# Attention and deformable attention in one kernel: three own taps in other units, the opening's loads on other queues, one late weight in later quarters

## The chip, the cores and the metric

The kernel runs on one core of a Trainium2 chip. Everything is float32. The metric is the device time of one execution in microseconds (us). A profile of one execution is read for the reasons: its span goes from the first to the last instruction. The engines are named PE (TensorE), DVE (VectorE), ACT (ScalarE), POOL (GpSimd) and SP (SyncE, which only issues DMAs). DMAs are issued from the queues of SP, ACT and POOL, each in its own program order.

## The reference

Two layers over `x` of 8 x 32 x 32 x 512, that is 8 batches of 1024 tokens with 512 channels:

```
# layer 0, per batch (seq = 1024 tokens, 8 heads of 64)
x_norm = group_norm(x)                        # 32 groups of 16 channels
q, k, v = split(x_norm @ w_qkv + b_qkv)
w   = softmax((q / 8) @ (k / 8).T)            # per head, 1024 x 1024
x   = x + (w @ v) @ w_out + b_out

# layer 1, per half batch of the reshaped image
x_ln = layernorm(x).transpose(0, 3, 1, 2)
q    = x_ln.reshape(...) @ wq + bq
o    = gelu(depthwise_conv_7x7_stride_2(q as an image) + dw_b)   # 49 taps a channel
off  = conv_1x1(o); grid = clip-free positions from tanh(off)
interp = bilinear samples of x at grid        # 256 points a batch
v = k = interp @ wv + bv
z   = softmax(qh @ kh.T) @ vh @ mo_w + mo_b + x       # heads of q, k, v by mq, mk, mv
out = gelu(layernorm(z) @ mlp_w + mlp_b) + z
```

## The kernel before

**Order.** Every instruction of an engine stands in the order in which the program issues it (the class `InOrder`, whose helper line, 54, is the line that most of the profile shows; tiles are therefore the names to go by). The order is written out by hand: `at(place, step)` puts a step on a list with a number as its due place, and `run_due(until)` runs all steps due before `until`, sorted by place and, where places are equal, by the order in which they were put down.

**Units.** Layer 0 is 256 units, 32 a batch (`per` = 32): a unit is one tile of 128 queries for one pair of heads. `push` (line 206) issues a unit: PE's scores into two `sc` tiles (`scores`, line 97), DVE's two row maxima `nmax`, ACT's two exponentials `e`; then the steps due before the unit's place 0.8; then DVE's two block transposes of `e` into `sq`; and, in odd units, sixteen DMAs on SP's queue that carry `sq` to `et` (`moved`, line 222); then the steps due before the next unit. There are two `sc` tiles, so the scores of a unit wait until ACT has read those of the unit before. The product of `et` with the values (`part`, tile `av`) follows three and four units after its odd unit. Units are numbered here from 0 to 31 within a batch, batches from 0 to 7.

**Work between.** The places around a batch hold the projections of q, k and v (`qkv_steps`, `value_steps`), the group norm of the next batch (`norm_steps`, line 582: `turn` transposes x into `xT`, `two_tiles` takes its statistics, `norm` applies them), and the output of the batch before (`out_steps`, line 739: on DVE `xr`, its statistics, `hat`; on POOL the sum with the bias and the two passes of `hat` over 128 x 512). In layer 0 there also runs the depthwise convolution of layer 1 for batches 0 to 5 (`EARLY` = 6): `conv_chunk` (line 950) does one block of 128 channels of one batch, and `conv_plan` (line 1000) says in which units its 49 taps fall. A row `(44, 6, 3)` means: in unit 44, counted from the start of the batch behind the block's own (so unit 12 of the batch after that), six taps by ACT and POOL (ACT scales into `part_x`, POOL adds to `oa`) and three by DVE alone (a SCALAR_TENSOR_TENSOR on `od`). DVE's own taps are due at 0.86 of their unit, so they come after the transposes of `sq` and ahead of the next unit's `nmax`. The blocks with own taps in the units that the change touches are the second (`cb` = 1, units 1 to 8) and the third (`cb` = 2, units 10 to 16) of each of those six batches; these parts of both run in batches 2 to 7.

**Opening.** Batch 0 has its eight tiles of x in two rows (lines 532 to 537): the first four, which are turned first, come by POOL's queue, the other four by SP's. The three thirds of `w_qkv` go to `wA` (queries), `wB` (keys) and `wC` (values), all by SP's queue, keys first (lines 547 and 548). The list `first_norm_places` (line 1032), shifted by -100, orders the first group norm; `warm(3)` (line 1050) puts matmuls without use at two places between. The squares of x for batch 1 (`load_squares`, line 523, four DMAs of 64 KB a tile, on POOL's queue) are due at `places[t] + 0.001`, right behind the first two turns (line 684); `load_weight(w_out)` on POOL's queue follows at -72.5.

**End of layer 0.** In batch 7 `fold_steps` (line 831) multiplies weights of layer 1 together. `load_quarter(w_out, c)` brings `w_out` back into the one tile `w` in four DMAs on ACT's queue at 25.2, 25.7, 26.2 and 26.7 (line 876); quarters of `mv_w` follow on the same queue at 27.2, 27.9, 28.6 and 29.3. The tile is read again at 33.1, after the last unit, by `out` of the last batch.

Of the kernel before, what the change touches and what calls it, by code (L numbers as in the profile page):

```python
# [17 lines left out]
P = 128  # L18
# [3 lines left out]
C = 512  # L22
NC = C // P
# [3 lines left out]
NQT = QB // P  # L27
NH = 8
HD = 64
# [219 lines left out]
def attention_then_deformable_attention(  # L249
# [30 lines left out]
    nc = tc.nc  # L280
    x_tok = x.rearrange("b h w c -> b (h w) c")
# [8 lines left out]
    ident = const.tile([P, P], F32, tag="ident", name="ident")  # L290
# [7 lines left out]
    def mm_tile():  # L298
        return ps_mm.tile([P, QB], F32, tag="mm", name="mm")
# [9 lines left out]
    def load_cols(pool, v, name):  # L309
        t = pool.tile([P, v.shape[0] // P], F32, tag=name, name=name)  # L310
        with nc.allow_non_contiguous_dma(reason="a vector onto partitions"):
            nc.sync.dma_start(t, v.rearrange("(c p) -> p c", p=P))
        return t
# [54 lines left out]
    def at(place, step):  # L368
        due.append((place, len(due), step))
# [40 lines left out]
    def kept(name):  # L410
        return keep.tile([P, NC, C], F32, tag=name, name=name)
# [98 lines left out]
    with ExitStack() as l0:  # L510
# [3 lines left out]
        nc = InOrder(tc)  # L514
        NX = 2
        NX_T = 3
        xs = {}
# [5 lines left out]
        def load_squares(b, t, r):  # L523
            if r == 0:
                xs[b, t] = work.tile([P, C], F32, tag="x", name="x", bufs=NX)
            nc.gpsimd.dma_start(
                xs[b, t][ts(r, SQ)].rearrange("q (s c) -> q s c", s=NSQ),
                x_tok[b][ts(t, P), ts(r, P)].rearrange("(s q) c -> q s c", s=NSQ),
            )
# [2 lines left out]
        x2 = work.tile([P, NC, QB], F32, tag="xT", name="x2", bufs=NX_T)  # L532
        for t in range(NQT):
            xs[0, t] = work.tile([P, C], F32, tag="attT", name="x0", bufs=NQB * NHP)
            nc.gpsimd.dma_start(xs[0, t], x_tok[0][ts(t, P), :])
            xs[0, NQT + t] = x2[:, t, :]
            nc.sync.dma_start(xs[0, NQT + t], x_tok[0][ts(NQT + t, P), :])
        w3 = [kept(name) for name in ("wA", "wB", "wC")]

        def load_runs(v, name):  # L540
# [3 lines left out]

        gsc, gbi = load_runs(gn_scale, "gsc"), load_runs(gn_bias, "gbi")
        bqkv = load_cols(wp, b_qkv, "bqkv")
        for i in (1, 0, 2):
            nc.sync.dma_start(w3[i], w_qkv.rearrange("(p c) o -> p c o", c=NC)[:, :, ts(i, C)])
        bout = load_row(wp, b_out, "bout")
        room_w = {}  # L550

# [5 lines left out]
        def load_quarter(w, c):  # L557
            if c == 0:
                room_w["w"] = work.tile([P, NC, C], F32, tag="w", name="w", bufs=1)
            nc.scalar.dma_start(room_w["w"][:, c, :], by_chunk(w)[:, c, :])  # L560
# [11 lines left out]
            out=g3, in_=g3, pattern=[[-span, ng], [0, span]], compare_op=ALU.is_ge,  # L572
# [3 lines left out]
            out=g3, in_=g3, pattern=[[span, ng], [0, span]], compare_op=ALU.is_ge,  # L576
# [5 lines left out]
        def norm_steps(b, start, places):  # L582
# [98 lines left out]
            if b + 1 < B:  # L681
                for t in range(NX):
                    for r, place in enumerate(square_places[NX + t]):
                        place = places[t] + 0.001 if b == 0 else place
                        at(start + place, lambda t=t, r=r: load_squares(b + 1, t, r))

        def qkv_steps(b, hp, places):

# [142 lines left out]
        def fold_steps(first):  # L831

            raws, wT = {}, {}

            rows = {}

            def row(name, dst, raw, vec):
                rows[name] = ByRow(dst, raws[raw], vec)

            def spare():  # L840
                return work.tile([P, NC, QB], F32, tag="xT", name="raw", bufs=NX_T)

            def fetch(name, w):
                raws[name] = spare()
                nc.gpsimd.dma_start(raws[name], by_chunk(w))

            def turn(name, m):
                if name == "v" and m == 0:
                    wT[name] = spare()
                src = room_w["w"] if name == "v" else raws["wq"]  # L850
                ps = mm_tile()
                for c in range(NC):
                    nc.tensor.transpose(ps[:, ts(c, P)], src[:, c, ts(m, P)], ident)
                nc.scalar.copy(wT[name][:, m, :], ps)

            def product(dst, tag, name, raw, i):
                if i == 0:
                    fold[dst] = kept(tag)
                ps = project(lambda m: wT[name][:, m, ts(i, P)], lambda m: raws[raw][:, m, :])
                nc.scalar.copy(fold[dst][:, i, :], ps)  # L860

            at(first + 18.3, number)
            for part in range(4):
                at(first + 18.35 + part, lambda part=part: load_biases(part))
            at(first + 19.3, set_refs)
            at(first + 17.7, lambda: load_weight(wv))
            at(first + 19.3, lambda: fetch("mk", mk_w))
            for m in range(NC):
                at(first + 23.5 + m // 2 + 0.05 * (m % 2), lambda m=m: turn("v", m))
            def quarter(name, w, c):  # L870
                if c == 0:
                    raws[name] = spare()
                nc.scalar.dma_start(raws[name][:, c, :], by_chunk(w)[:, c, :])

            for c in range(NC):
                at(first + 25.2 + 0.5 * c, lambda c=c: load_quarter(w_out, c))
                at(first + 27.2 + 0.7 * c, lambda c=c: quarter("mv", mv_w, c))
                at(first + per + 1.24 + 0.001 * c, lambda c=c: quarter("wq", wq, c))
            for i, place in enumerate((25.5, 27.5, 28.5, 29.5)):
                at(first + place, lambda i=i: product("wvk", "wC", "v", "mk", i))  # L880
            def row_tile():
                return work.tile([P, C], F32, tag="v", name="row_b", bufs=5)

            def col_tile():
                return work.tile([P, NC], F32, tag="mu", name="col", bufs=2)

            at(first + 24.65, lambda: row("k", bvk, "mk", bv_c))
            at(first + 24.651, lambda: rows["k"].away(row_tile(), nc.gpsimd))
            at(first + 27.9, lambda: rows["k"].back(col_tile(), nc.gpsimd))
            raws["wq"] = None  # L890

            for i, place in enumerate((30.5, 31.5, 32.5, 32.52)):
                at(first + place, lambda i=i: product("wvv", "wB", "v", "mv", i))
            last = first + per
            at(last + 0.6, lambda: wT.update(q=spare()))
            at(last + 2.41, lambda: rows["k"].add(nc.vector))
            at(last + 3.5, lambda: row("v", bvv, "mv", bv_c))
            at(last + 3.51, lambda: rows["v"].away(row_tile(), nc.scalar))
            at(last + 4.28, lambda: rows["v"].back(col_tile(), nc.scalar))
            at(last + 3.6, lambda: fetch("mq", mq_w))  # L900
            for m in range(NC):
                at(last + 4.27 + 0.001 * m, lambda m=m: turn("q", m))
            for i in range(NC):
                at(last + 4.5 + 0.01 * i, lambda i=i: product("wqq", "wA", "q", "mq", i))
            at(last + 4.48, lambda: row("q", bqq, "mq", bq_c))
            at(last + 4.481, lambda: rows["q"].away(row_tile(), nc.scalar))
            at(last + 4.515, lambda: rows["q"].back(col_tile(), nc.scalar))
            for name in ("v", "q"):
                at(last + 4.9, lambda name=name: rows[name].add(nc.vector))
# [40 lines left out]
        def conv_chunk(b, cb, n):  # L950
# [34 lines left out]
            for unit, by_scalar, by_vector in counts:  # L985
# [15 lines left out]
            (20.5, (24.3, 25.3),  # L1001
             ((26, 3, 2), (27, 4, 2), (28, 6, 3), (29, 6, 3), (30, 6, 2), (31, 6, 2), (32, 3, 1)), 32),
            (26.3, (32.3, 32.6),
             ((33, 6, 2), (34, 6, 2), (35, 4, 0), (36, 6, 3), (37, 4, 0), (38, 5, 0), (39, 4, 0),
              (40, 5, 2)), 41),
            (33.6, (41.3, 41.6),
             ((42, 6, 3), (43, 5, 1), (44, 6, 3), (45, 5, 1), (46, 5, 1), (47, 4, 0), (48, 6, 3)), 49),
            (42.6, (49.3, 49.6),
             ((50, 6, 2), (51, 6, 3), (52, 6, 3), (53, 5, 2), (54, 4, 1), (55, 4, 1), (56, 4, 2)), 56),
        ]  # L1010
# [39 lines left out]
        def warm(n):  # L1050
            out = mm_tile()
            for c in range(n):
                for m in range(2):
# [3 lines left out]
                        start=(c == 0), stop=(c == n - 1),  # L1057
                    )

        norm_steps(0, -100, first_norm_places)  # L1060
        for place in (-76.035, -74.5):
            at(place, lambda: warm(3))
        at(-72.5, lambda: load_weight(w_out))
# [15 lines left out]
        for b in range(B):  # L1079
            first = b * per  # L1080
            for hp in range(1, NHP):
                places = first_places if b == 0 else pair_places
# [20 lines left out]
            for hp in range(NHP):  # L1103
                for qt in range(NT):
                    n = first + hp * NT + qt
                    if n % per == 0 and b > 0:
# [6 lines left out]
                        if b + 1 == B:  # L1113
                            places = [last_places(B * per, t) for t in range(NT)]
                            out_steps(b, attT, places, last=True)
                    t = qkv[b, hp]
# [4 lines left out]
                        at=qt % NQT,  # L1121
# [8 lines left out]
    with ExitStack() as l1:  # L1130
        nc = tc.nc


        def pool(name, bufs=1):
            return l1.enter_context(tc.tile_pool(name=name, bufs=bufs, reuse_waits="tile"))

        late, late2, cv, cvhat, first, raw, wp = (
            pool(n) for n in ("late", "late2", "cv", "cvhat", "first", "raw", "w2")
        )
        work = pool("work1", 2)  # L1140
        nc = InOrder(tc)
# [404 lines left out]
        for hi in range(2 * B):  # L1546
            if hi > 1:
                for c, place in enumerate((-0.35, 0.65, 1.3, 1.65) if hi % 2 else (-0.7, 1.3, 1.65, 1.7)):
                    place = -1.03 if hi == 2 and c == 0 else place
# [39 lines left out]
```

## Time and profile before

| | |
|---|---|
| three runs | 3268.69, 3271.52 (median), 3274.23 us |
| the profiled execution | 3270.55 us, of which the span is 3268.8 us |
| layer 0 | about 34.6 to 2104 us of the span |
| busy | PE 3215.1, DVE 2544.7, ACT 1766.2, POOL 1633.5 us |
| DMA | 674.30 MB, mean 206 GB/s |
| first tile of x turned; first projection starts | 7.12; 23.30 us |
| PE's idle time, by what ended most of it | `sc` on ACT's `e` 10.8; `av` on the DMA into `et` 9.5; on the DMA of x 7.6 us |

How to read it: PE is busy nearly all the time, so the time is PE's own work plus the stretches in which it waits. A stretch is told by the interval between the starts of two units' scores (`sc<-k,q`). A unit takes PE 7.19 us without, and 10.62 us with a second projection, where nothing holds it up. A wait shorter than the drain of a matmul does not show as idle time, only as a longer interval.

### The profile page before, as it was taken

How to read it: one execution, taken by the hardware profiler on the slowest of the kernel's cores; microseconds unless marked ns; L12 is line 12 of the kernel's file. 1: busy time of each engine (PE TensorE's matmuls, PEld its weight loads, DVE VectorE, ACT ScalarE, POOL GpSimd, SP SyncE). 2: the span in 40 equal slices, each digit the busy share in tenths (PEclk: the TensorE clock that was granted, in tenths of full speed). 3: DMA queues.
4: the chain of work that ended last, by engine and by line, in shares of the span. 5: the costliest groups of instructions: out<-in, count | busy, mean ns of one | idle time of the engine just before them, and what ended most of it. 6: DMA issues, size and time to landing. Idle time of an engine off the chain costs nothing.

```text
span 3268.8 us, 59474 instructions
## 1 busy us (share of the span) xinstructions
PE 3215.1 (98%) x21476; PEld 1299.1 (40%) x21476; DVE 2544.7 (78%) x3493; ACT 1766.2 (54%) x3798; POOL 1633.5 (50%) x2110
## 2 busy tenths in 40 slices
PE   8999999999999999999999999999999999999999
PEld 4344444344344444444434434333333333333333
DVE  5777878898888888888888888457868687676765
ACT  3443356566567567557557656235555555554442
POOL 2002316755755765665674677225556565643323
PEclk9999999999999999999999999999999999999999
DMA  6666776777776776776676677678777786877874
GB/s 173 165 177 170 206 182 185 210 194 190 210 190 181 208 200 174 204 211 178 184 231 171 177 217 209 175 227 264 223 242 241 227 264 213 259 257 230 268 234 132
DMA packets 479900, 674.30 MB, mean 206 GB/s; under 512 B 77404, under 2 KB 269208, under 8 KB 479352
## 3 DMA queue, kind: packets, MB, share of 16 engines
q1 hardware_dynamic: 433760, 529.53, 56.6%
q0 software_dynamic: 42480, 136.79, 13.7%
q10 hardware_dynamic: 3368, 4.20, 0.4%
q8 instruction: 170, 2.79, 0.4%
q14 instruction: 122, 1.00, 0.1%
HBM read 263.17 MB, written 138.69 MB: 123 GB/s over the span
## 4 chain that ended last, share of the span: by engine, by line
PE 78%; ACT 5%; DVE 5%; POOL 5%; DMA 3%; issue 2%; SPq 1%; POOLq 0%; DVEq 0%; ACTq 0%
PE mm L54 49%; PE sc L54 15%; PE av L54 14%; ACT e L54 3%; POOL oa L54 2%; SPq L54 1%; DVE sq L54 1%; DVE nmax L54 1%; ACT part_x L54 1%; POOL xr L54 1%; DMA et<-sq_d 1%; POOL hat L54 1%; DMA et<-sq 1%; DVE chunk L54 1%; DMA sq_d<-sq 0%
## 5 line engine op out<-in xcount | busy, mean ns | idle before, releaser
L54 ACT ACTIVATE e<-sc,nmax 128x1024 f32<-128x1024 f32 (+1 forms) x1024 | 801.7, 796 | 534.7 <-DVE nmax L54 531.1
L54 DVE TENSOR_REDUCE nmax<-sc 128x1 f32<-128x1024 f32 (+1 forms) x640 | 749.5, 1212 | 272.1 <-PE sc L54 267.5
L54 POOL TENSOR_TENSOR oa<-part_x,oa 128x256 f32<-128x256 f32 x852 | 637.3, 748 | 534.9 <-ACT part_x L54 490.3
L54 DVE STREAM_TRANSPOSE sq<-e 128x1024 f32<-128x1024 f32 x640 | 764.1, 1224 | 119.9 <-ACT e L54 100.7
L54 ACT ACTIVATE part_x<-pad_x,dww_x 128x256 f32<-128x256 f32 x852 | 441.6, 545 | 282.4 <-POOL oa L54 280.5
L54 PE MATMUL sc<-k,q 64*64 64x512 f32 x4096 | 519.9, 602 | 12.3 <-ACT e L54 9.8
L54 PE MATMUL av<-et,v 128*64 128x256 f32 x4096 | 499.8, 386 | 16.4 <-DMA et<-sq 9.5
L54 PEld LDWEIGHTS av<-et,v 128*64 128x64 f32 x4096 | 274.9, 137 | 332.1 <-issue 159.2
L54 PEld LDWEIGHTS sc<-k,q 64*64 64x64 f32 x4096 | 140.5, 132 | 331.9 <-issue 214.4
L54 POOL TENSOR_TENSOR chunk<-parts,chunk 128x256 f32<-128x256 f32 x240 | 185.3, 772 | 137.2 <-ACT parts L54 123.5
L54 POOL TENSOR_TENSOR mv<-mv,minus_half 128x1 f32<-128x1 f32 x128 | 75.8, 593 | 327.7 <-DVE mv L54 326.6
L54 PE MATMUL mm<-wo,attH 128*64 128x512 f32 x1024 | 233.7, 598 | 0.0
L54 PE MATMUL mm<-wC,xT 128*64 128x256 f32 x2048 | 232.2, 379 | 0.0
L54 PE MATMUL mm<-xT,wB 128*64 128x512 f32 x1024 | 230.8, 592 | 0.6 <-DVE xT L54 0.6
L54 PE MATMUL mm<-hat_h,wA 128*64 128x512 f32 x1024 | 230.9, 593 | 0.0
L54 PE MATMUL mm<-xT,wA 128*64 128x512 f32 x1024 | 230.7, 592 | 0.0
L54 PE MATMUL mm<-w,attT 128*64 128x512 f32 x1024 | 230.1, 592 | 0.0
L54 DVE SCALAR_TENSOR_TENSOR od<-pad_x,dww_x,od 128x256 f32<-128x256 f32 x276 | 223.5, 810 | 5.5
L54 PE MATMUL mm<-wm,zT 128*64 128x512 f32 x976 | 220.7, 592 | 0.5 <-ACT zT L54 0.5
L54 ACT ACTIVATION_READ_ACCUMULATOR e<-sc,nmax 128x1 f32 x1024 | 209.6, 205 | 0.0
L54 POOL DMA_DIRECT2D x<-in_x_dram x144 | 80.5, 561 | 248.6 <-DVE xT L54 125.8
L54 PEld LDWEIGHTS mm<-wC,xT 128*64 128x64 f32 x2048 | 148.6, 137 | 77.1 <-issue 6.4
(200 smaller groups left out, 3590.5 us busy)
## 6 DMA issues: line engine op xcount, KB each, us to landing
et<-sq SPq DMA_DIRECT2D x2048, 128.0 KB
sq_d<-sq SPq DMA_DIRECT2D x128, 512.0 KB
et<-sq_d SPq DMA_DIRECT2D x128, 512.0 KB
inv<-rs_d SPq DMA_DIRECT2D x250, 128.0 KB
xr<-mid POOLq DMA_DIRECT2D x64, 256.0 KB
xr<-in_x_dram POOLq DMA_DIRECT2D x62, 256.0 KB
out_dram<-res POOLq DMA_DIRECT2D x60, 256.0 KB
zn_d<-zn SPq DMA_DIRECT2D x57, 256.0 KB
```

The lines of the kernel that those rows point to most:

```text
L54: return self.tc.keep_in_program_order(op(*args, **kwargs))
```

## The change

The change has five parts.

1. `conv_plan`: DVE's own taps move. In the second block one tap goes from unit 40 to unit 38 (batch units 8 and 6). In the third, one goes from unit 44 and two from unit 48 (batch units 12 and 16), two go to unit 45 and one to unit 47 (13 and 15). Each block keeps its 49 taps and its taps by ACT and POOL.
2. The first four tiles of x come by SP's queue, the other four by POOL's.
3. `wB` is loaded by ACT's queue, at -83.54, right behind the turn of the fourth tile; SP's queue keeps `wA` and `wC`, in this order.
4. The squares of x for batch 1 are due at -70, behind `load_weight(w_out)`; five pairs of small matmuls on the identity (`warm_ident`) come ahead of everything else on PE.
5. In batch 7 the quarters of `w_out` are due at 29.7, 30.2, 30.7 and 31.2.

```diff
--- before.py
+++ after.py
@@ -532,9 +532,9 @@
         x2 = work.tile([P, NC, QB], F32, tag="xT", name="x2", bufs=NX_T)
         for t in range(NQT):
             xs[0, t] = work.tile([P, C], F32, tag="attT", name="x0", bufs=NQB * NHP)
-            nc.gpsimd.dma_start(xs[0, t], x_tok[0][ts(t, P), :])
+            nc.sync.dma_start(xs[0, t], x_tok[0][ts(t, P), :])
             xs[0, NQT + t] = x2[:, t, :]
-            nc.sync.dma_start(xs[0, NQT + t], x_tok[0][ts(NQT + t, P), :])
+            nc.gpsimd.dma_start(xs[0, NQT + t], x_tok[0][ts(NQT + t, P), :])
         w3 = [kept(name) for name in ("wA", "wB", "wC")]
 
         def load_runs(v, name):
@@ -544,8 +544,12 @@
 
         gsc, gbi = load_runs(gn_scale, "gsc"), load_runs(gn_bias, "gbi")
         bqkv = load_cols(wp, b_qkv, "bqkv")
-        for i in (1, 0, 2):
-            nc.sync.dma_start(w3[i], w_qkv.rearrange("(p c) o -> p c o", c=NC)[:, :, ts(i, C)])
+
+        def load_qkv(i, queue):
+            queue.dma_start(w3[i], w_qkv.rearrange("(p c) o -> p c o", c=NC)[:, :, ts(i, C)])
+
+        for i in (0, 2):
+            load_qkv(i, nc.sync)
         bout = load_row(wp, b_out, "bout")
         room_w = {}
 
@@ -681,8 +685,8 @@
             if b + 1 < B:
                 for t in range(NX):
                     for r, place in enumerate(square_places[NX + t]):
-                        place = places[t] + 0.001 if b == 0 else place
-                        at(start + place, lambda t=t, r=r: load_squares(b + 1, t, r))
+                        place = -70 if b == 0 else place
+                        at(place + start * (b > 0), lambda t=t, r=r: load_squares(b + 1, t, r))
 
         def qkv_steps(b, hp, places):
 
@@ -873,7 +877,7 @@
                 nc.scalar.dma_start(raws[name][:, c, :], by_chunk(w)[:, c, :])
 
             for c in range(NC):
-                at(first + 25.2 + 0.5 * c, lambda c=c: load_quarter(w_out, c))
+                at(first + 29.7 + 0.5 * c, lambda c=c: load_quarter(w_out, c))
                 at(first + 27.2 + 0.7 * c, lambda c=c: quarter("mv", mv_w, c))
                 at(first + per + 1.24 + 0.001 * c, lambda c=c: quarter("wq", wq, c))
             for i, place in enumerate((25.5, 27.5, 28.5, 29.5)):
@@ -1001,10 +1005,10 @@
             (20.5, (24.3, 25.3),
              ((26, 3, 2), (27, 4, 2), (28, 6, 3), (29, 6, 3), (30, 6, 2), (31, 6, 2), (32, 3, 1)), 32),
             (26.3, (32.3, 32.6),
-             ((33, 6, 2), (34, 6, 2), (35, 4, 0), (36, 6, 3), (37, 4, 0), (38, 5, 0), (39, 4, 0),
-              (40, 5, 2)), 41),
+             ((33, 6, 2), (34, 6, 2), (35, 4, 0), (36, 6, 3), (37, 4, 0), (38, 5, 1), (39, 4, 0),
+              (40, 5, 1)), 41),
             (33.6, (41.3, 41.6),
-             ((42, 6, 3), (43, 5, 1), (44, 6, 3), (45, 5, 1), (46, 5, 1), (47, 4, 0), (48, 6, 3)), 49),
+             ((42, 6, 3), (43, 5, 1), (44, 6, 2), (45, 5, 3), (46, 5, 1), (47, 4, 1), (48, 6, 1)), 49),
             (42.6, (49.3, 49.6),
              ((50, 6, 2), (51, 6, 3), (52, 6, 3), (53, 5, 2), (54, 4, 1), (55, 4, 1), (56, 4, 2)), 56),
         ]
@@ -1057,7 +1061,19 @@
                         start=(c == 0), stop=(c == n - 1),
                     )
 
+        def warm_ident(n):
+            out = mm_tile()
+            for c in range(n):
+                for m in range(2):
+                    half = ds(m * HD, HD)
+                    nc.tensor.matmul(
+                        out[half, 0:P], lhsT=ident[:, half], rhs=ident,
+                        start=(c == 0), stop=(c == n - 1),
+                    )
+
         norm_steps(0, -100, first_norm_places)
+        warm_ident(5)
+        at(-83.54, lambda: load_qkv(1, nc.scalar))
         for place in (-76.035, -74.5):
             at(place, lambda: warm(3))
         at(-72.5, lambda: load_weight(w_out))
```

## The prediction

> **What bounds the kernel now.** I read the page first, then PE's waits, then the chain of waits around the units that the change touches, then PE's and the queues' own timelines at both ends of layer 0.
>
> ```profile
> span 3268.8 us, 59474 instructions
> ...
> PE 3215.1 (98%) x21476; PEld 1299.1 (40%) x21476; DVE 2544.7 (78%) x3493; ACT 1766.2 (54%) x3798; POOL 1633.5 (50%) x2110
> ```
>
> PE has 53.7 us of idle time in all (span less busy), so no part of the change can win much; it can lose more. Three places matter. First the opening, in PE's timeline (start, length, both in us):
>
> ```profile
> 7.12 1.10 PE L54 MATMUL mm<-ident,x 128*128 128x128 f32 x4 [7.12 <-DMA x<-in_x_dram]
> 8.39 2.37 PE L54 MATMUL mm<-ident,x 128*128 128x128 f32 x8 [0.17 <-DMA x<-in_x_dram]
> 11.08 4.51 PE L54 MATMUL mm<-ident,x 128*128 128x128 f32 x20 [0.31 <-DMA x<-in_x_dram]
> ...
> 23.30 1.08 PE L54 MATMUL mm<-xT,wB 128*64 128x512 f32 x4 [0.64 <-DVE xT L54]
> ```
>
> PE turns a tile as it lands: 7.12, 8.39, 9.64 and 11.08 us. The four tiles that come by SP are there when the last of POOL's is, so five tiles (20 transposes) run without a break. Everything to 23.30 follows the last turn.
>
> Second, units 13 to 16. This is the chain in batch 4 (start, length); units 13 to 17 start at 1145.85, 1156.47, 1167.09, 1174.28 and 1181.48:
>
> ```profile
> 1159.02 1.11 DVE xT L54
> 1160.13 1.12 DVE nmax L54
> ...
> 1161.27 2.33 ACT e L54 x4
> ...
> 1177.75 1.31 DVE stats L54 x4
> 1179.06 1.14 DVE nmax L54
> ...
> 1180.22 2.34 ACT e L54 x4
> ...
> 1182.61 1.94 PE sc L54 x14
> ```
>
> DVE ends unit 13's late work with `xT`, starts unit 14's `nmax` with no gap, ACT's `e` waits for that, ACT's and POOL's taps and the passes of `hat` run behind `e` with hardly a gap, then come `e` of unit 15, `sq`, `xr`, the statistics, `nmax` of unit 16, `e`, and PE's scores of unit 17. PE pays there:
>
> ```profile
> 1181.48 3.07 PE L54 MATMUL sc<-k,q 64*64 64x512 f32 x16
> ```
>
> 3.07 us in place of 1.95: 1.12 lost inside the group, more where its start is late too (unit 16 takes 7.79 in batch 2 and 8.09 in batch 5, in place of 7.19). The own taps of unit 16 come after that `nmax`, so they aren't in this chain; those of unit 13 are, and a tap in unit 15 would be.
>
> Third, the end of layer 0 in PE's timeline, and SP's waits in the stretch around it (total, times, longest):
>
> ```profile
> 2064.00 3.46 PE L54 MATMUL av<-et,v 128*64 128x256 f32 x16 [3.60 <-DMA et<-sq]
> ...
> 2081.14 1.95 PE L54 MATMUL av<-et,v 128*64 128x256 f32 x16 [1.01 <-DMA et<-sq]
> ```
>
> ```profile
> SPq L54 <- DMA raw<-in_L_conv_mv_w_dram: 7.4, 2, 6.8
> SPq L54 <- DMA w<-in_L_conv_w_out_dram: 4.8, 2, 4.2
> ```
>
> SP stands still in the middle of a group of `et` DMAs until a weight quarter issued by ACT has landed. In unit 28 this costs PE 12.54 us in place of 7.19: 3.60 of waiting, the rest because the granted clock then is 0.57 for some 3.5 us.
>
> **The taps.** Six batches have them (2 to 7). A DVE tap takes 0.48 us free (unit 14, batch 2), 0.62 when the end of a POOL pass falls on it (unit 13), and 1.26 when POOL's passes of `hat` lie over it (three in 3.78 us, unit 16 of batch 3).
>
> Unit 13, plus two: they stand between `mv` and `xT`, where DVE has no gap. POOL then issues a DMA and does one tiny power (632.69 to 633.86 in batch 2), so they run nearly free: 2 x 0.50 = 1.0. Unit 14 is 10.62 long and absorbs this for PE (`e` ends some 7.4 us into it), but not for the chain, since the POOL run starts from that `e` (POOL idle 1.92 until ACT).
>
> Unit 15, plus one: place 0.86 ties with `two_tiles`, put down earlier, so it comes after the statistics, directly ahead of `nmax`; a pass of `hat` is under way. Between 0.48 and 1.26, I take 0.65, near the 0.62 row, because in batch 2 only a rest of the pass is left: it ends at 653.34, and DVE arrives at 653.16.
>
> Unit 12, minus one: `e` of unit 13 waits for POOL's run, so little comes back: POOL's bias pass took 1.45 under three taps and takes 1.27 else, 0.2. Bounds: nothing, or the whole tap, 0.8. Units 8 and 16, minus one and two: nothing. After unit 8, unit 12 waits for `et` of unit 9, which SP issues at 1125.13 while `sq` had ended at 1122.3; after unit 16, `nmax` of 17 stands in a unit with a second projection, whose last `e` ends 1 us before PE asks for it already now. Unit 6, plus one: DVE idles before the next `nmax`, which waits for PE's scores; if that cover is gone it costs at most 1.3 a batch.
>
> Per batch 1.0 + 0.65 - 0.2 = 1.45, six times 8.7 us. Ends: 6 x (3 x 0.48 - 0.8) = 3.8, and 6 x 3 x 1.26 = 22.7.
>
> [...]
>
> **The opening.** Removed: SP's late start for `wB` and eight issues of squares (4.4 us of POOL's queue) behind POOL's tiles, so 512 KB less beside the weights. Moved: SP issues its first tile at 0.80, so tiles 1 to 4 land first; POOL's four keep their issue times (1.41 to 4.1) and I let them land as now, the last at 11.08. Added: ten small matmuls before x, in time in which PE idles. One tile then remains to be turned after 11.08 instead of five: 4.51 - 1.1 = 3.4 us. ACT, which copies each tile (0.59), first issues `wB`. SP takes 1.18 for `wC` and 3.25 for `wB`; a quarter takes ACT 0.33, so four parts 1.3. It falls after the fourth copy, near 10 us, and holds up four copies: the last ends near 13.6 instead of 16.2. Statistics are then DVE's run of two pairs (2 x 1.41): gain 2.2. Ends: 3.4, and a loss of 1 if `wB` comes too late. It shares with `wA`, `wC` and three rows on SP's queue; at half of 260 GB/s (the windows from 12 to 17 us) 1 MB needs 8 us from 10.5 and is due at 21, so there are 2 us to spare. Queued behind the issue on ACT: copies 5 to 8, and PE's last turns, as three `mm` tiles are all there are. The squares go past one small power and `w_out` on POOL's queue, land near 30 and are due at 41.4.
>
> **The quarters.** Without them SP's group of unit 25 isn't held (4.8 us), lands before 2060.4, and unit 28 takes 7.19: a gain of 5.35. Unit 30 then waits some 0.3 for the `mv` quarter instead of 1.01. But the quarters now stand among the group of unit 29, in the same pattern four units later. That group (2078.00 to 2088.6) is due at 2093.7, 2.5 us after it lands; a hold of 4.8 would put 2.3 back, and with the `mv` quarter ahead of it some more. I take 2.7 back: net -5.35 - 0.7 + 2.7 = -3.3. Ends: nothing back, -6.1; all back with a slow stretch of the clock, +1.5. The issues (0.33 each) fall in gaps of ACT of 1.6 us and more. The last quarter is due at 2104.4 and goes out near 2086: covered.
>
> **Sum.** 3270.55 + 8.7 - 2.2 - 3.3 = 3273.75 for the profiled execution, which lies 0.97 under the median of the runs: 3274.7, so 3275 us. What I can't tell from no change is 0.2%, 6.5 us either way (the three runs spread over 5.5).
>
> **The rivals.** *Slower:* the three taps cost what the contended rows say, 0.62 twice and 1.26, with nothing back from unit 12: 2.5 x 6 = 15.0, and unit 29's group gives back nearly all that unit 28 wins, with the opening at -1.5: 3271.5 + 15 - 1.5 - 0.5 = 3284.5. For it: `hat` passes lie at 1177 to 1181 and POOL has few gaps in unit 15. It decides once a tap in these units takes over 0.75. Against: POOL's two free stretches in unit 13. *Faster:* the taps fit in slack that I don't see (the chain is inferred from the release times), and both ends come full: 3271.5 - 2.2 - 6.1 = 3263.2. For it: batches 4 and 6 have 0.5 to spare in unit 15. Against: unit 17 loses over 1.1 in every one of the batches 2 to 6. *Nothing moves:* taps are covered and the quarters' hold is merely moved to unit 32: 3270, as the opening alone.
>
> **How the numbers follow.** Forecast 0.42, its own range 3268 to 3278; slower rival 0.35; faster 0.19; nothing moves 0.04. The range takes in most of the rivals: 3264 to 3286. Over 0.2% faster is below 3265, over 0.2% slower above 3278: chances 0.19, 0.45 and 0.36.
>
> **What would show it.** Right: in batches 2 to 6 the interval from unit 13's start to unit 18's start grows by 1.2 to 1.8 us, with `sc` of unit 16 or 17 stretched, and unit 17's `nmax` early without use; the first projection starts near 21; unit 28 takes 7.19 and `av` waits for `et` behind unit 31. Wrong: these intervals unchanged or shorter; `wB` releasing PE's first projection; ACT's copies not held at all.

## The result and the profile after

The change made the kernel slower: 3292.24 us median (3287.87 to 3297.88, five runs) against 3271.52 us, ratio 1.0065 with a 95% interval of 1.0049 to 1.0081. The forecast was 3275, with a range up to 3286. The profiled execution of the changed kernel takes 3291.24 us, 20.7 more than that of before. By stretches between the starts of units' scores:

| stretch | after less before, us |
|---|---|
| start to the first scores | -0.9 |
| batches 0 and 1 | -0.1 |
| batches 2 to 6 | +13.5 (2.5 to 2.9 each) |
| batch 7, units 0 to 30 | -4.0 (unit 28 -5.2, unit 30 -1.1) |
| unit 31 to layer 1's first scores | +9.7 |
| layer 1 | +2.5 |

The head of the page and the first line of its busy times (engine, us, share, instructions):

```profile
span 3289.5 us, 59505 instructions
...
PE 3227.9 (98%) x21496; PEld 1300.1 (40%) x21496; DVE 2530.0 (77%) x3493; ACT 1765.3 (54%) x3798; POOL 1633.9 (50%) x2110
```

PE's idle time is 61.6 us (span less busy), only 7.9 more than before. The other 12.8 are in PE's busy time: the matmuls on the identity (2.4), which stand where PE was idle before and cost no time, and groups of matmuls that take longer (10.4), because they wait inside the group or run at a lower clock. In the scores of unit 17 of batch 4 before, PE counts as busy for 3.01 of 3.07 us, though the group takes 1.95 where nothing holds it: two matmuls, 0.64 and 0.59 us on record, fill the first 1.1. Whoever looks only at idle time misses half of the loss.

**The opening**, in PE's timeline (start, length, what is done, idle time ahead and its releaser) and in the chain of waits between 18 and 24 us:

```profile
8.84 4.45 PE L54 MATMUL mm<-ident,x 128*128 128x128 f32 x24 [1.93 <-DMA x<-in_x_dram]
...
17.76 2.80 PE L54 MATMUL mm<-xT,ident 128*64 128x512 f32 x12
22.39 3.65 PE L54 MATMUL mm<-xT,wB 128*64 128x512 f32 x16 [1.83 <-DMA wB<-in_L_conv_w_qkv_dram]
```

```profile
10.83 11.42 DMA wB<-in_L_conv_w_qkv_dram
```

PE ends the last matmul ahead of the first projection at 20.56, in the kernel before at 22.66: up to there 2.1 us are won. There the projection starts 0.64 us behind that matmul, when DVE's first tile of the normed `xT` is done; in the changed kernel that tile is done at 21.15, so the projection could have begun near 21.2. It starts at 22.39, because `wB` was 11.42 us on its way: 1.2 of the 2.1 us are lost again.

**Units 13 to 17**, batch 4. DVE's late work of unit 13 and what follows, changed kernel:

```profile
1162.53 2.61 DVE L54 SCALAR_TENSOR_TENSOR od<-pad_x,dww_x,od 128x256 f32<-128x256 f32 x3
1165.06 1.13 DVE L54 STREAM_TRANSPOSE xT<-x 128x512 f32<-128x512 f32 x1
1166.12 2.30 DVE L54 TENSOR_REDUCE nmax<-sc 128x1 f32<-128x1024 f32 x2
```

and the same place in the kernel before:

```profile
1158.47 0.61 DVE L54 SCALAR_TENSOR_TENSOR od<-pad_x,dww_x,od 128x256 f32<-128x256 f32 x1
1159.01 1.12 DVE L54 STREAM_TRANSPOSE xT<-x 128x512 f32<-128x512 f32 x1
```

From the first tap to `xT` it is 2.53 us instead of 0.54: two more taps cost 1.99, not 1.0. The single taps take 0.69, 0.48 and 1.36, and the third takes 1.36 or 1.37 in each of the six batches. What lies over it is in POOL's timeline of the changed kernel:

```profile
1163.47 0.68 POOL L54 TENSOR_TENSOR mv<-mv,minus_half 128x1 f32<-128x1 f32 x1
1164.13 2.40 POOL L54 TENSOR_TENSOR oa<-part_x,oa 128x256 f32<-128x256 f32 x3
```

POOL's quiet stretch (a DMA issue and the tiny power) ends at 1164.13, and the third tap, which starts at 1163.77, runs into the next pass. The profile's chain view names a DMA as what released `xT` in both kernels; but `xT` starts 0.08 us ahead of the recorded end of the last tap in both, so it is the taps that it follows. PE pays in the scores of units 16 and 17:

```profile
1178.66 3.04 PE L54 MATMUL sc<-k,q 64*64 64x512 f32 x16 [1.15 <-ACT e L54]
...
1188.17 3.07 PE L54 MATMUL sc<-k,q 64*64 64x512 f32 x16 [1.15 <-ACT e L54]
```

Before, unit 16's scores took 1.95 with no wait in front, and unit 17's 3.07 with none in front either. Now both have 1.1 inside the group and 1.15 ahead of it.

**The end of layer 0**, PE's timeline:

```profile
2098.58 3.60 PE L54 MATMUL mm<-raw 128*64 128x512 f32 x16
2105.01 3.30 PE L54 MATMUL av<-et,v 128*64 128x256 f32 x16 [2.82 <-DMA et<-sq]
...
2181.58 4.90 PE L54 MATMUL mm<-smp,wC 128*64 128x256 f32 x22 [4.79 <-DVE smp L54]
```

and two stretches right behind these two waits (stretch, its length, busy time of PE, PEld, DVE, ACT and POOL, granted clock, share of the DMA engines, GB/s):

```profile
2104.50:2107.50 3.00, 2.50 (x12) 1.65 (x14) 0.00 (x0) 0.00 (x0) 0.00 (x0) 0.50 0.78 211
2180.00:2185.00 5.00, 3.42 (x16) 1.91 (x18) 1.49 (x2) 0.47 (x1) 0.00 (x0) 0.50 0.93 356
```

Each wait is followed by a stretch at half clock (3.4 us from 2104.38, 6.8 from 2179.47). The 9.7 us of this part are then 2.5 (2.82 in place of 0.30) + 1.4 (half of the 2.8 us in which PE works in the first stretch; the group of `av` takes 3.30 in all, 1.95 at full clock) + 3.35 (4.79 in place of 1.44) + 2.4 (half of the 4.7 us in which it works in the second) = 9.65. SP's waits between 2086 and 2106 (total, times, longest) show who delayed `et`:

```profile
SPq L54 <- DMA raw<-in_L_conv_mv_w_dram: 3.6, 1, 3.6
SPq L54 <- DMA w<-in_L_conv_w_out_dram: 2.0, 1, 2.0
```

The longer wait for the samples, 2.1 ms behind the edits of the opening, was in no step of the prediction.

### The profile page after: what moved, and what is told of

It reads as the page before. It is cut to its first block, busy times and chain, and to the rows that moved or that the text cites. A ratio compares the mean times of both kernels' runs of the same rounds, so it can differ in the third digit from the quotient of the medians.

```text
span 3289.5 us, 59505 instructions
## 1 busy us (share of the span) xinstructions
PE 3227.9 (98%) x21496; PEld 1300.1 (40%) x21496; DVE 2530.0 (77%) x3493; ACT 1765.3 (54%) x3798; POOL 1633.9 (50%) x2110
## 4 chain that ended last, share of the span: by engine, by line
PE 79%; DVE 5%; DMA 5%; ACT 4%; POOL 3%; SPq 2%; issue 2%; POOLq 0%; DVEq 0%; ACTq 0%
PE mm L54 49%; PE sc L54 15%; PE av L54 15%; ACT e L54 3%; SPq L54 2%; DMA et<-sq 1%; DVE nmax L54 1%; DVE sq L54 1%; DMA et<-sq_d 1%; POOL oa L54 1%; POOL hat L54 1%; DMA sq_d<-sq 1%; DVE chunk L54 1%; POOL xr L54 0%; ACT part_x L54 0%
## 5 line engine op out<-in xcount | busy, mean ns | idle before, releaser
L54 PE MATMUL sc<-k,q 64*64 64x512 f32 x4096 | 527.8, 602 | 22.5 <-ACT e L54 19.9
L54 PE MATMUL av<-et,v 128*64 128x256 f32 x4096 | 499.6, 386 | 10.5 <-DMA et<-sq 8.7
L54 DVE SCALAR_TENSOR_TENSOR od<-pad_x,dww_x,od 128x256 f32<-128x256 f32 x276 | 209.9, 761 | 5.1
```

Of the source, the lines that this page charges most:

```text
L54: return self.tc.keep_in_program_order(op(*args, **kwargs))
```

## The experiments

All started from the kernel before or the changed one. Times against the kernel before, measured beside it:

| kernel | what it is | ratio, 95% interval |
|---|---|---|
| taps | part 1 of the change alone | 1.0060 (1.0045 to 1.0075) |
| opening | parts 2 to 4 alone | 1.0028 (1.0019 to 1.0037) |
| quarters | part 5 alone | 1.0000 (0.9991 to 1.0008) |
| opening_room | opening, buffers at their old addresses | 1.0014 (1.0005 to 1.0022) |
| after_room | the whole change, old addresses | 1.0045 (1.0031 to 1.0058) |
| opening_squares | opening, squares at their old place | 1.0017 (1.0008 to 1.0026) |
| opening_sp | that, with `wB` on SP's queue | 1.0005 (0.9996 to 1.0014) |
| quarters_pool | old places, GpSimd's queue | 1.0011 (1.0001 to 1.0022) |
| quarters_spread | one quarter a unit | 0.9996 (0.9987 to 1.0005) |
| tap14 | unit 13's own tap moved to unit 14 | 0.9998 (0.9989 to 1.0008) |
| pool13 | both chains of unit 13 shortened | 0.9983 (0.9974 to 0.9992) |
| two13, one15 | the moves into unit 13 and 15, each alone | one run each: 3280.01, 3271.68 us (before: 3267.96) |
| opening_room_2 | opening_room once more, for a second trace | one run: 3269.78 us (before: 3269.41) |

The three parts alone add up to 1.0088 (half width 0.002, from the three intervals), the whole to 1.0065 (half width 0.0016); the difference is within the two half widths.

**The taps.** *taps* has the `conv_plan` part of the diff and nothing else.

> The kernel before with the change's taps alone (both blocks). Theory: the taps carry most of the loss by themselves. In the profile of the changed kernel batches 2 to 6 are 2.5 to 2.9 us longer each and units 13 to 17 of batch 7 1.3; so +13 to +16 us here. Unit 13's three own taps take 0.69, 0.48 and 1.36 us, and the wait of layer 1's first keys for the samples stays at about 1.4 us. Rival A, the forecast's term: +8.7 us. Rival B: a good part of the change's loss comes from the other queues, and the taps alone cost under 6 us.

The other three change one row each, third block:

```diff
-((42, 6, 3), (43, 5, 1), (44, 6, 3), (45, 5, 1), (46, 5, 1), (47, 4, 0), (48, 6, 3))
+((42, 6, 3), (43, 5, 1), (44, 6, 3), (45, 5, 3), (46, 5, 1), (47, 4, 0), (48, 6, 1))   two13
+((42, 6, 3), (43, 5, 1), (44, 6, 2), (45, 5, 1), (46, 5, 1), (47, 4, 1), (48, 6, 3))   one15
+((42, 6, 3), (43, 5, 1), (44, 6, 3), (45, 5, 0), (46, 5, 2), (47, 4, 0), (48, 6, 3))   tap14
```

> The kernel before with only the two taps of the third block moved from unit 16 to unit 13. In the change's profile the three own taps of unit 13 take 0.69, 0.48 and 1.36 us, where the one tap took 0.62: the third falls under a pass of POOL. Theory: these 1.91 us stand whole in the chain, so the stretch from unit 12's start to unit 18's start grows by 1.7 to 2.0 us in each of the batches 2 to 6. Rival, the forecast's price: 1.0 us a batch. Second rival: the chain has slack and the stretch grows by under 0.5.

> The kernel before with only the one tap of the third block moved from unit 12 to unit 15. Theory: the stretch from unit 12's start to unit 18's start grows by 0.3 to 0.7 us a batch (the tap takes 0.47 to 0.71 in the change's profile, ahead of unit 16's row maximum). Rival: unit 12's three taps are in the chain too, and the stretch stays the same or gets shorter.

> The kernel before with the one own tap of unit 13 moved on to unit 14 (45 to 46). If the chain through unit 13's late work sets units 14 to 17, taking its tap away must win: unit 14's tap takes 0.48 and is followed by idle time before unit 15's row maximum. Theory: the stretch from unit 12's start to unit 18's start is 0.5 to 0.7 us shorter in batches 2 to 6, 3 to 4 us in all, ratio near 0.999. Rival: another chain takes over at once, and nothing changes (under 0.2 us a batch).

Measured: the stretch from unit 12's start to unit 18's start, kernel before in us, the others as the difference from it:

| | batch 2 | 3 | 4 | 5 | 6 | 7 | sum |
|---|---|---|---|---|---|---|---|
| before | 56.25 | 55.98 | 55.97 | 55.99 | 55.76 | 54.73 | |
| after | +2.04 | +2.34 | +2.67 | +1.85 | +2.84 | +1.32 | +13.1 |
| taps | +2.33 | +2.30 | +2.38 | +2.34 | +2.89 | +1.48 | +13.7 |
| two13 | +1.68 | +2.16 | +1.66 | +1.68 | +1.90 | +2.57 | +11.7 |
| one15 | +0.12 | +0.39 | +0.70 | +0.45 | +0.87 | +0.07 | +2.6 |
| tap14 | -0.08 | +0.14 | -0.29 | -0.39 | +0.05 | -0.49 | -1.1 |
| opening | -0.04 | +0.26 | +0.04 | -0.05 | +0.26 | +0.32 | +0.8 |

*taps* came out at 3286.24 us, 17 over before (15 to 24 by the ratio's interval), at or above what was expected; its profiled execution is the fastest of its six, with layer 1 at -4.2 for no reason that I know. Unit 13's taps take 0.68, 0.48 and 1.36 there, and the wait for the samples is 1.85.

So the taps alone make the loss of these units, and two13 and one15 together (14.3) make that of the taps (13.7). The second block's tap, in units 6 and 8, lies outside this stretch; but batches 2 to 6 as a whole are 12.4 us longer in *taps*, and the stretch has 12.2 of that, so next to nothing is left for it. The two taps in unit 13 are most of the loss. What the whole time of *taps* has beyond these 13.7 no trace assigns. The stretch must be read from unit 12 on: unit 12's wait for `et` of unit 9 went away in the changed kernel (batch 4: -1.41) and I took this for a gain, but it also went in *opening*, which has the old taps (batch 4: unit 12 -0.88, units 13 to 17 +0.92). It is a wait that the next units absorb or hand back, worth nothing by itself.

two13 and tap14 together show that adding a tap to unit 13 costs all of it while taking one away wins next to nothing (0.2 us a batch in the mean). The chain of waits in tap14, around unit 13 of batch 4 (start, length, what):

```profile
1150.58 0.70 POOL oa L54
...
1151.30 0.56 ACT part_x L54
1151.85 2.19 ACT e L54 x4
1154.05 0.43 ACT part_x L54
...
1154.54 0.74 POOL oa L54
```

It does not pass through `xT` any more. POOL's passes and ACT's `part_x` and `e` in turn make a second chain, of nearly the same length. *pool13* takes a tap from that one too:

```diff
-((42, 6, 3), (43, 5, 1), (44, 6, 3), (45, 5, 1), (46, 5, 1), (47, 4, 0), (48, 6, 3))
+((42, 6, 3), (43, 5, 1), (44, 6, 3), (45, 4, 0), (46, 5, 2), (47, 4, 0), (48, 6, 4))
```

> Taking unit 13's own tap away won nothing, because a second chain, POOL's passes and ScalarE's exponentials in turn, ends within 0.3 us of the first. Here both are shortened: third block (45, 4, 0), (46, 5, 2), (48, 6, 4), so one tap of ScalarE and POOL less in unit 13 and one own tap more in unit 16, where VectorE's taps are not followed by anything urgent. Theory: the stretch from unit 12's start to unit 18's start gets 0.4 to 1.0 us shorter in batches 2 to 6; 2 to 5 us in all, ratio 0.9985 to 0.9995. Rival: unit 17's row maximum, now 1.4 us later, holds unit 18's scores and gives it back: stretch unchanged within 0.3.

Measured: the stretch is 0.40, 0.89, 0.41, 0.44, 0.31 and 1.27 us shorter in batches 2 to 7, 3.7 in all, and the ratio 0.9983: 3264.91 us median against 3271.43 beside it. Batch 6 falls short of the 0.4 that was expected; the ratio is a little better than the 0.9985 to 0.9995 that was, and what it has beyond the 3.7 us is not assigned. So two chains of nearly one length bound these units, and this version beats both kernels. A kernel that shortens the second chain alone was not run.

**The opening.** *opening* is the change without parts 1 and 5. *opening_room* and *after_room* set the squares' two buffers aside where the old order did it:

```diff
-            if r == 0:
+            if r == 0 and (b, t) not in xs:
                 xs[b, t] = work.tile([P, C], F32, tag="x", name="x", bufs=NX)
...
+        def hold_x(t):
+            xs[1, t] = work.tile([P, C], F32, tag="x", name="x", bufs=NX)
+
+        for t in range(NX):
+            at(first_norm_places[t] - 100 + 0.001, lambda t=t: hold_x(t))
         norm_steps(0, -100, first_norm_places)
```

> The kernel before with the change's opening alone: queues of x, keys' weights on ScalarE's queue, squares behind the output weight, matmuls on the identity. Theory: the first projection starts 0.9 us earlier, and 3.4 us are lost 2.1 ms later, because the squares' buffers are now set aside after the small tiles of the norm, so that a gather buffer of layer 1 comes to lie on a small tile that is still in use: PE waits about 4.8 us for the samples instead of 1.4, the second gather starts some 8.7 us behind the first instead of 1.8. Sum +2 to +5 us. Rival: the longer wait for the samples belongs to the quarters or the taps; then this kernel gains 0.5 to 1.5 us and the wait stays at 1.4.

> The same opening, with the squares' two buffers set aside at the old point of the order, and nothing else moved. Theory: the wait for the samples is back at about 1.4 us, the second gather follows the first by 1.8; -0.5 to -2 us against before and about 3.4 us less than the opening without this. Rival: no difference between the two.

Why an order of buffers matters: the pool hands out addresses as its tags are first asked for. In the compiled programs (bytes in each partition):

```
                  small tiles mu/col       second gather buffer of layer 1   the second gather waits for
before            105408 and 105440        99456 to 101503                   hat (DVE), earlier
after, opening    101312 and 101344        99456 to 101503                   bqq <- col (DVE), late
```

With the squares' 4 KB asked for later, `mu`, whose place `col` uses at the end of layer 0, moves down into what becomes a gather buffer, and the gather must wait until `col` has been read. POOL's timeline in *opening*:

```profile
2146.57 1.53 POOL L54 DMA_INDIRECT row<-mid,ii  x1 [0.33 <-issue]
2155.28 0.97 POOL L54 DMA_INDIRECT row<-mid,ii  x1 [7.19 <-DVE smp L54]
```

and in *opening_room*:

```profile
2149.36 1.53 POOL L54 DMA_INDIRECT row<-mid,ii  x1 [0.33 <-issue]
2151.19 0.97 POOL L54 DMA_INDIRECT row<-mid,ii  x1 [0.30 <-DVE hat L54]
```

The second gather follows the first by 8.71 us or by 1.83, and PE's wait for the samples is 4.83 or 1.42. The ratios differ by 0.0014, 4.6 us (half width about 4). Over all 16 traces the wait is 4.8 us in the two kernels with the moved addresses (*opening* and the change) and 0.6 to 2.0 in the fourteen others. The profile names `smp` as the releaser of the 7.19; the program has the wait on `bqq`, which DVE ends just ahead of it.

> The whole change, with the squares' two buffers set aside at the old point of the order, so that all buffers have the addresses of before. Theory: PE waits 1 to 1.9 us for the samples at the start of layer 1 instead of 4.8, no stretch at half clock follows there, and the time falls by 4 to 7 us against the changed kernel: 12 to 17 us over before (ratio 1.0037 to 1.0052). Rival: the wait for the samples comes from the late end of layer 0 (the quarters) and stays over 3 us; then the ratio stays at 1.006 or more.

Here the wait for the samples is 2.00 in place of 4.79, a little over what was expected, and one stretch at half clock still follows it. The time is 3285.76 us, ratio 1.0045 and not 1.0065: 6.5 us less than the change, with a half width of about 7; the wait itself is the surer sign. The rival, that the quarters' late end causes the wait, falls.

Even with the old addresses the opening stays 4.6 us (1.6 to 7.2) over before. The next three runs looked for why.

```diff
-                        place = -70 if b == 0 else place
-                        at(place + start * (b > 0), lambda t=t, r=r: load_squares(b + 1, t, r))
+                        place = places[t] + 0.001 if b == 0 else place
+                        at(start + place, lambda t=t, r=r: load_squares(b + 1, t, r))
...
-        for i in (0, 2):
+        for i in (1, 0, 2):
             load_qkv(i, nc.sync)
...
-        at(-83.54, lambda: load_qkv(1, nc.scalar))
```

*opening_squares* has the first of these edits on the opening, *opening_sp* both.

> The change's opening (x by the other queues, keys' weights by ScalarE, matmuls on the identity) with the squares of batch 1 left at their old place behind the first two turns. Open: the opening with its buffers at the old addresses still measured 4.6 us over before (1.6 to 7.2), though its first projection starts 3 us earlier. Theory 1: the late squares are the cause (GpSimd's transfers then meet the weights and the first units), and this kernel is 1 to 3 us faster than before. Theory 2: the swap of the queues alone shifts later races (the small row of sums against a 256 KB read of x in batch 1), and this kernel stays 2 to 6 us over before, with a wait of over 2 us for et in unit 12 of batch 1.

> The same, but with the keys' weights left on SP's queue ahead of the queries' (so of the opening only the queues of x and the matmuls on the identity remain). Theory: the keys' weights are what the first projection waited for in the changed kernel (1.83 us); by SP's queue they land earlier, and the first projection starts at 20.2 to 21.0 instead of 22.4 in the changed kernel and 23.3 in the kernel before. Rival: the loads share the same bandwidth, and they land no earlier (over 21.5). For the whole time: theory 1 gives 2 to 3 us faster than before, theory 2 of the run before stays over it.

> The opening with the old addresses once more, for a second trace. If theory 2 holds, unit 12 of batch 1 again waits 2 us or more for et; if that was chance, it waits under 1.3 us as in the kernel before.

The first projection starts at 22.13 in opening_squares, after 3.88 us of waiting for `wB`: with the squares beside it, `wB` is 13.26 us on its way, against 10.9 to 11.4 in four traces without, so moving them was right for `wB`. With `wB` on SP's queue it starts at the earliest of all traces:

```profile
19.95 3.65 PE L54 MATMUL mm<-xT,wB 128*64 128x512 f32 x16 [0.64 <-DVE xT L54]
```

So the queue chosen for `wB` was what cost the start. But none of the three is faster than before as a whole: 1.0017 and 1.0005, and 3269.78 us in the one run of opening_room_2. Theory 1 falls. Theory 2 is not settled: unit 12 of batch 1 waits for `et` 2.18, 2.56, 1.62 and 2.01 us in opening, opening_room, opening_room_2 and after_room, but 0.25 in the changed kernel, and 1.37 in opening_squares. In the first four batch 1 is 3.2 to 4.1 us longer than before, in the changed kernel not (-0.1); but *quarters_pool*, with the old opening, has +3.1 there too. One more thing the traces show is that the start itself varies: the first projection begins between 21.04 and 23.72 in nine executions with the old opening (mean 22.4; the kernel before's 23.30 was a late one), and between 20.36 and 22.39 in five with the change's (mean 21.3). The gain at the start is nearer 1.1 than 3 us. One small loss goes with `wB` on ScalarE's queue: PE waits 1.5 us ahead of unit 25 of batch 0 in all six traces that have it so, 1.2 in the ten others, and in three of the six a stretch at half clock follows, in one of the ten. More of the loss can be read from the granted clock on record for every execution: its mean is 0.99758 in the twelve of *opening_room* and 0.99843 in the 28 of before. The difference is worth, by my estimate, 2.8 us of a span of 3270 (half width 1.5), of the 5.0 between the mean times; *opening_squares* has 2.8 of 6.1 by the same sum. So by this estimate about half of it is time at half clock, more of it than before. Which waits bring that about, and what the other half is, stays open.

**The quarters.** *quarters* is part 5 alone. *quarters_pool* keeps their old places and changes the queue (`nc.gpsimd.dma_start` for `nc.scalar.dma_start` in `load_quarter`). *quarters_spread*:

```diff
-at(first + 25.2 + 0.5 * c, lambda c=c: load_quarter(w_out, c))
-at(first + 27.2 + 0.7 * c, lambda c=c: quarter("mv", mv_w, c))
+at(first + 25.79 + c, lambda c=c: load_quarter(w_out, c))
+at(first + (27.791, 28.791, 28.792, 29.79)[c], lambda c=c: quarter("mv", mv_w, c))
```

> The kernel before with the late quarters of the output weight alone. Theory: unit 28 is 5.2 us shorter and unit 30 1 us, but the group of et behind unit 31 is held by a quarter, PE waits 2.8 us for it and then runs some 3.4 us at half clock: net -1 to +1 us. Rival A, the forecast's term: -3.3 us. Rival B: the hold in the changed kernel comes from the later taps, and here the quarters win 6 us.

> The kernel before with the four late quarters of the output weight at their old place, but issued by GpSimd's queue. SP's et DMAs and ScalarE's DMAs use the same eight semaphores in turn, and a DMA waits for the last one on its semaphore to land; GpSimd's have eight of their own. Theory: SP's group behind unit 25 is not held any more, unit 28 takes 7.2 us in place of 12.5, and no wait of 2 us or more appears for et behind units 29 and 31: 5 to 6 us less. Rival A: it is the DMA engines' bandwidth that held the group; then unit 28 still takes over 9 us. Rival B: GpSimd's issues hold up its passes of hat in units 25 to 30, which gives back over 3 us.

> The kernel before with the late quarters spread out: output weight at 25.79, 26.79, 27.79 and 28.79, mv weight at 27.79, 28.79, 28.79 and 29.79, so that each is issued by ScalarE ahead of an odd unit's transposes or between two groups, and has landed when SP comes to the DMA that waits on the same semaphore. Theory: no hold over 1 us, unit 28 takes 7.2 us, unit 30 7.2 to 7.5, no wait for et behind unit 31: 6 us less, ratio near 0.998. Rival: each 256 KB read slows the et transfers wherever it stands; then the sum of waits for et in units 28 to 31 stays over 2.5 us and the ratio at 0.9995 to 1.001.

*quarters*: unit 28 is 5.36 us shorter, unit 31 and what follows 4.35 longer, with this row of PE's in between:

```profile
2093.81 2.84 PE L54 MATMUL av<-et,v 128*64 128x256 f32 x16 [2.87 <-DMA et<-sq]
```

The trace's net is -1.0, the measured ratio 1.0000: the hold is moved, not removed. *quarters_pool* was to remove it, since in the trace of before the 2982 DMAs of SP and the 20 of ACT count on the same eight semaphores (100 and 109 to 115), and GpSimd's 553 on eight others (101 to 108). Unit 28 still waits, and SP's waits between 2045 and 2072 name another reason:

```profile
2069.97 3.00 PE L54 MATMUL av<-et,v 128*64 128x256 f32 x16 [3.24 <-DMA et<-sq]
```

```profile
SPq L54 <- DMA et<-sq: 6.2, 5, 3.4
```

No weight holds SP now; SP waits for its own earlier `et` DMAs to land, 3.4 us at the longest, and unit 28 takes 12.2 us. That is the sign that rival A named. The DMAs of unit 25's group take 9.2 us (median) from issue to landing here, and 5.9 in *quarters*, where no `w_out` runs beside them: 1 MB of weights slows the group's transfers from GpSimd's queue too. That it is bandwidth they share is an inference. *quarters_spread* has one quarter a unit, and the waits are still there:

```profile
2062.01 1.95 PE L54 MATMUL av<-et,v 128*64 128x256 f32 x16 [1.54 <-DMA et<-sq]
...
2080.02 3.68 PE L54 MATMUL av<-et,v 128*64 128x256 f32 x16 [3.56 <-DMA et<-sq]
```

1.54 + 3.56 = 5.1 us, in units 28 and 30. By these numbers and the ratio its rival holds; but SP's waits between 2036 and 2090 show that the hold by the weights is still there, so this run does not tell it from slowed transfers:

```profile
SPq L54 <- DMA w<-in_L_conv_w_out_dram: 11.3, 3, 5.8
```

No place or queue tried wins anything that can be measured.

## Why the prediction was wrong

**The taps, +8.7: the mechanism was right, the size was not.** The chain runs through unit 13's `xT` as forecast, and the loss shows at the scores of units 16 and 17. The step that failed is "POOL then issues a DMA and does one tiny power (632.69 to 633.86 in batch 2), so they run nearly free: 2 x 0.50 = 1.0". The stretch of 1.17 us holds the first two of three taps; I had priced the added taps one by one and not laid all three into the gap. Measured: 1.99 on DVE in batch 4, and 1.7 to 2.6 in the stretch in *two13*. The sign it named, the interval from unit 13's start to unit 18's growing by 1.2 to 1.8, came out at 1.9 to 4.1 in batches 2 to 6 (from unit 12 on, 1.9 to 2.8). The other two terms hold in the mean: 0.65 for unit 15 less 0.2 for unit 12 is 0.45, and *one15* measured 0.43, but in a single trace and from 0.07 to 0.87; unit 15's tap took 0.47 to 0.72. Six batches then make 13.1 in the changed kernel and 13.7 in *taps*, near the slower rival's 15.0, and for the reason the rival gave: "It decides once a tap in these units takes over 0.75", and one takes 1.36. The upper end of this term, 22.7, has each of the three taps at 1.26; of the two added in unit 13 one ran nearly free at 0.48, and one, with the start of POOL's pass over it, took 1.36.

**The opening, -2.2: under half of it, and a cost that was not in the sum.** The step "1 MB needs 8 us from 10.5 and is due at 21, so there are 2 us to spare" failed: it took 11.42 us from 10.83 and was due near 21.2, as forecast. The sign that the prediction named against itself, `wB` releasing PE's first projection, is there, and so is the other one: ACT's copies were not held (each of the last four follows the one before by 0.27 us, as before). The larger error is that the squares' move was priced only by its due time ("land near 30 and are due at 41.4"). It also changed the order in which buffers are set aside, and through that the wait for the samples in layer 1. In the changed kernel's trace it is 5.7 us, the longer wait and the half clock behind it; *opening* against *opening_room* says 4.6 us, *after_room* against the change 6.5.

**The quarters, -3.3: the mechanism was right, the give-back was too small.** Unit 28 takes 7.3 as forecast, unit 30 is 1.1 shorter, and `av` behind unit 31 waits for `et` because the group of unit 29 is held. The step that was mis-sized is "I take 2.7 back": it was 3.9 in the changed kernel, 2.5 of longer waiting and 1.4 because the clock is then half for 3.4 us. I had seen that same price in unit 28, where I put 5.35 and not 3.60 on the gain, but had it in the loss only at the far end of the range (+1.5).

**The sum.** From the two traces: taps 13.1, start -0.9, quarters -5.2 - 1.1 + 3.9 = -2.4, the samples 5.7 (3.35 + 2.4), together 15.5 of the 20.7. Against the forecast's 8.7, -2.2, -3.3 and nothing for the samples, the largest misses are the samples' 5.7 and the taps' 4.4. Of the rest, 2.5 are in layer 1, which in the other traces differs from before by -4.2 to +5.2; 1.3 are a wait in unit 11 of batch 5, and 1.0 is in units 20 and 21 of batch 7. No experiment assigned these to an edit, so a quarter of the loss has no shown cause.

## What to carry to other kernels

Lay all instructions of a busy stretch into the gap that is to hide them, with the next engine's pass behind it, before pricing any of them as free; and look for the second chain of the same length, because then, as here, a tap added costs its whole time and a tap removed wins next to nothing until both chains are shortened (over six batches +11.7 us for two taps more a batch, -1.1 for one less, -3.7 with both chains shortened). Moving a first use of a buffer can move the addresses of a whole pool, and with them false waits in a stage far away (here 4.8 us for the samples in place of 1.4), so compare addresses and waits of the compiled programs, not only the edited lines. A stall of some 2 us or more has to be priced with the half-clock stretch that mostly follows here (behind 43 of 45 windows with 2.0 us or more of idle time), on the side of the loss as on that of the gain.

## What the runs showed of the hardware

**Half clock followed windows of 3.413 us with idle time in them.** In each of the 16 traces (before, after and 14 experiments) the granted clock changes on a grid of 3.413 us (before: to 0.50 at 2064.26 and at 2234.93, fifty steps apart, and back to 1.00 at 2067.68), at a phase that differs from run to run (after: to 0.50 at 2104.38, 11.75 steps behind the 2064.26 of before). I divided each trace along its grid, from 30 us on, and counted PE's idle time in every window at full clock:

| PE idle in one window | windows | next window at half clock |
|---|---|---|
| 2.0 us or more | 45 | 43 |
| 1.7 to 2.0 | 16 | 2 |
| 1.2 to 1.7 | 60 | 6 |
| 0.9 to 1.2 | 77 | 0 |

From this table I estimate that a wait of about 2 us costs up to 1.7 more (half of a window) if it falls into one window, and mostly nothing if the grid divides it between two: 8 of the 153 windows with 0.9 to 2.0 us of idle time have half clock behind them. It may be one way in which equal programs differ by several us from one execution to the next: of the 27 executions of the kernel before that were measured beside *quarters_spread*, the one with a granted clock of 1.000 took 3263.73 us, the two with 0.997 took 3271.71 and 3272.81.
